# Dividing an attention's output instead of its weights, with sums from products with ones, and a retimed schedule, in a fused attention, delta-rule and feed-forward kernel

## The chip, the cores and the metric

The kernel runs on one core of one Trainium2 chip. A core has a matrix engine (PE, whose weight loads the profile shows as PEld), a vector engine (DVE), a scalar engine (ACT), a general engine (POOL), an engine that issues transfers (SP), and 16 DMA engines. The metric is device microseconds of one execution, the median over the runs; less is better.

## The reference

The input is 16 sequences of 128 tokens with 256 features. Two residual steps follow each other; all arithmetic is in float32.

```python
x = x + delta_rule(attention(x, cond_1, Wq, Wk, Wv, Wo), W_qkv, W_z, ...)
x = x + ffn(lora_ffn(x, Wg, Wu, Wd, adapters[itok]), gate_w, up_w, down_w, ...)

# attention: 16 heads of 16 features, causal
q, k, v = (proj(x, W) for W in (Wq, Wk, Wv))
q = q * minimum(cond_1, 4.0)
attn = softmax(where(causal, q @ k.T / sqrt(16), lowest), axis=-1)
return (attn @ v) @ Wo.T

# delta_rule: 16 key heads and 32 value heads of 128 features, chunks of 64 tokens:
# projections, a causal convolution of 4 taps, silu, norms of q and k, running sums of the
# gates, the inverse of a unit lower triangular 64 x 64 matrix per chunk and value head,
# values, outputs, a norm of the outputs, silu(z), and the product with W_out
```

The change lies in the softmax of `attention` and in the times at which the steps of all of the first residual step are placed.

## The kernel before

**Two levels of work.** The 16 sequences form 4 groups of 4 (`GS`). Attention (`attention`) runs on a group: `project` makes queries, keys and values, `block(g, i, e)` handles one sequence `i` and one half `e` of the features, which is 8 of the 16 heads, and `output` makes the group's result `hT`, its gates' logarithms (`logs`) and their running sums (`running`). There are 8 blocks in a group and 32 in all. The delta rule runs on 64 units, one for a key head and a group.

**One block.** `product` makes the scores of 8 heads in two PSUM tiles (L241). `mask` scales and masks them on DVE (L246), `largest` takes the maxima on DVE (L251), `less` subtracts them on POOL (L254), `exp` runs on ACT (L257). `total` sums the rows and takes reciprocals on DVE (L261, L262), and `share` divides the weights by multiplying them with those on POOL (L265). `turn` transposes the weights on PE by halves (L272) and copies them with ACT (L273). `weigh` multiplies values and weights (L280): four products of 32 columns each, which write the four blocks of 32 partitions of one PSUM tile. Each holds two heads, of which every partition needs one; `pick` chooses it with an ACT copy scaled by `even` and a DVE operation with `odd` (L287, L288).

**Times, and who obeys them.** Every step is a Python function with a time. Steps are sorted by time and called in this order, and then a scheduler of the framework, which has a model of durations of its own, makes each engine's instruction order from it. On the chip every engine takes its instructions strictly in that order. The unit of attention's times is one block: the steps of block b stand at b plus the twelve numbers of its list, for instance 2.2 for the first `turn`. Steps before `ALONE` = 11.2 run before anything else; the rest is spread over the first beats of the delta rule, `PACE` = 3.9 blocks to a beat. A beat is 24 units of the table `TIMES`; with each beat one new unit enters. A step at time t of `TIMES` runs in beat t // 24 after its unit entered, at t % 24.

**What is in a steady beat.** The steps of several units stand in one beat: `keys` of the newest (projections L437, convolution L446 and L448, SiLU L533, squares L469, norms L475), `decays` (L549, L553), `mergers` and `last` (which join the inverses of small blocks: L696 to L735), `values` (L437 again, L754), `outputs`: the gate (L771), `new_values` (L782, copied to `y` by ACT at L783), `attend` for two heads (L788, its square on ACT at L792, its product with the gate on DVE at L794) and `root` (L801, L803); and `finish` (POOL's L823, then L832 on PE). ACT's `exp` of `aT` stands at L511. For every four units `inverse` inverts 128 blocks of 32 by 32 on DVE and POOL, by rows (L587, L589), eights (L612, L616) and sixteens (L597 on POOL, L647 and L649 on DVE), spread over two beats. From beat 7 on the mergers and values need the memory that attention's tiles held, so attention ends before it.

**First loads.** SP's queue issues `wk`, the first group of `x` (`load_xT(0)`) and `wq` one after the other, ACT's queue the small ones.

The lines of the profile are those of this file:

Of the kernel before, what the change touches and what calls it, by code (L numbers as in the profile page):

```python
# [8 lines left out]
F32 = mybir.dt.float32  # L9
I32 = mybir.dt.int32  # L10
AF = mybir.ActivationFunctionType
ALU = mybir.AluOpType
AX = mybir.AxisListType
PSUM = bass.MemoryType.PSUM

P = 128
NB = 16
S = 128
D = 256
NT = NB * S  # L20
ND = D // P
NG = 4
GS = NB // NG
GT = GS * S
# [10 lines left out]
BL = 32  # L35
BLOCKS = tuple(slice(BL * b, BL * (b + 1)) for b in range(P // BL))
# [20 lines left out]
def tile_adaln_attn_ffn(  # L57
# [8 lines left out]
    nc = tc.nc  # L66
    V, A, G, T = nc.vector, nc.scalar, nc.gpsimd, nc.tensor
# [77 lines left out]
    HB = P // HD  # L145
    GB = GS * ND

    def attention():
# [22 lines left out]
        def load_xT(g):  # L171
            xTs[g] = p1.tile([P, ND, GT], F32, name="xT_sb", tag="xT")
            nc.sync.dma_start(out=xTs[g], in_=xT.rearrange("(c p) t -> p c t", p=P)[:, :, g * GT : (g + 1) * GT])

        nc.sync.dma_start(out=wk_sb, in_=wkT.rearrange("(c p) e -> p c e", p=P))
        load_xT(0)
        nc.sync.dma_start(out=wq_sb, in_=wqT.rearrange("(c p) e -> p c e", p=P))
        nc.scalar.dma_start(out=pr, in_=prec.rearrange("b o -> (b o)").partition_broadcast(P))
        nc.sync.dma_start(out=wv_sb, in_=wvT.rearrange("(c p) e -> p c e", p=P))
        nc.sync.dma_start(out=wo_sb, in_=woT.rearrange("(c p) e -> p c e", p=P))  # L180
# [50 lines left out]
        def block(g, i, e):  # L231
# [12 lines left out]
            def mask(n):  # L244
                b = g * GS + i
                V.scalar_tensor_tensor(out=d["s"][:, n], in0=d["ps"][n], scalar=pr[:, b : b + 1],  # L246
                                       in1=causal[:, None, :].to_broadcast([P, 4, S]), op0=ALU.mult, op1=ALU.add)
# [8 lines left out]
            def exp():  # L256
                A.activation(d["s"], d["s"], AF.Exp)  # L257

            def total():
                d["sm"] = p1.tile([P, HB], F32, name="sm", tag="sm")  # L260
                V.tensor_reduce(out=d["sm"], in_=wide(d["s"]), axis=AX.X, op=ALU.add)  # L261
                V.reciprocal(d["sm"], d["sm"])  # L262

            def share():
                G.tensor_tensor(wide(d["s"]), wide(d["s"]), d["sm"][:, :, None].to_broadcast([P, HB, S]), ALU.mult)  # L265

            def turn(n):
                if n == 0:
                    d["pT"] = p1.tile([P, 2, 4, S], F32, name="pT", tag="pT", bufs=1)
                ps = ps_b.tile([P, 4, S], F32, name="ps_pt", tag="b")  # L270
                for j in range(4):
                    T.transpose(ps[:, j, :], d["s"][:, n, j, :], ident)  # L272
                A.copy(d["pT"][:, n], ps)  # L273

            def weigh():

                d["po"] = ps_r.tile([P, 2, S], F32, name="ps_o", tag="r")
                for r, b in enumerate(BLOCKS):
                    c0 = e * P + r * BL
                    T.matmul(d["po"][b], lhsT=grp[g]["v"][:, i, c0 : c0 + BL],  # L280
                             rhs=d["pT"][:, r // 2, 2 * (r % 2) : 2 * (r % 2) + 2, :], start=True, stop=True)

            def pick():
                if i == e == 0:
                    grp[g]["oT"] = p1.tile([P, ND, GT], F32, name="oT", tag="oT", bufs=1)
                oT = grp[g]["oT"][:, e, cols]
                A.activation(oT, d["po"][:, 0, :], AF.Copy, scale=even)  # L287
                V.scalar_tensor_tensor(out=oT, in0=d["po"][:, 1, :], scalar=odd, in1=oT, op0=ALU.mult, op1=ALU.add)  # L288

            return [product, lambda: mask(0), lambda: mask(1), largest, less, exp, total, share,  # L290
                    lambda: turn(0), lambda: turn(1), weigh, pick]

        def output(g):

# [57 lines left out]
        def plan(t0, fs, times):  # L352
            steps.extend((t0 + t, len(steps) + i, f) for i, (t, f) in enumerate(zip(times, fs, strict=True)))

        for g in range(NG):
            t0 = GB * g
            plan(t0, project(g), [-2, -1.8, -1, -0.8, -0.6, -0.4] if g == 0 else [-6.55, -5.55, -4.55, -3.55, -2.85, -1.85])
            for i in range(GS):
                for e in range(ND):
                    plan(t0 + ND * i + e, block(g, i, e), [0, 0.15, 0.3, 0.45, 0.5, 1.0, 1.05, 1.45, 2.2, 2.45, 2.6, 2.8])  # L360
            plan(t0 + GB, output(g), [2.15, 2.45, 3.0, 3.6])
        return sorted(steps, key=lambda t: t[:2])


# [506 lines left out]
    def residual(g, t):  # L871
# [10 lines left out]
        "sums": [16.5],  # L882
        "decays": [42.5, 44.5, 48.5],
        "inverse": [4.0, 5.0, 6.0, 7.0, 8.0, 9.0, 10.0, 11.0, 12.0, 17.0, 17.0, 21.0, 23, 26, 25, 28, 27, 30, 29, 32, 34, 36, 36, 38, 38, 40, 40, 43, 46, 50],
        "mergers": [179, 180.5, 189.0],
        "last": [193.0],
        "values": [175.5, 179.5, 182, 186.5, 194, 195],
        "outputs": [217, 219, 224, 224, 227, 230, 232.5, 237],
        "finish": [244, 249.5, 255.5],
        "logs": [18],  # L890
    }
# [4 lines left out]
    LOG = TIMES["logs"][0]  # L896
    next_log = lambda name, i: int((TIMES[name][i] - LOG) // BEAT) + 1

    ALONE, PACE = 11.2, 3.9
    load_qk(units[0])  # L900
    ahead = attention()
    while ahead and ahead[0][0] < ALONE:
# [3 lines left out]
    def plan(n, steps, times):  # L906
        for f, t in zip(steps, times, strict=True):
            k = n + int(t // BEAT)
            planned.setdefault(k, []).append((t - BEAT * (k - n), len(planned[k]) if k in planned else 0, f))
# [279 lines left out]
```

## Time and profile before

| | |
|---|---|
| median of 3 runs | 2310.58 us (2308.94 to 2312.5) |
| the profiled execution: its time | 2318.2 us |
| its span, first to last instruction | 2316.5 us |
| busy: PE, DVE, ACT, POOL | 2137.0, 1360.2, 1363.9, 895.4 us |
| mean granted PE clock | 0.968 of full |
| first product of PE | at 12.15 us |
| first projection of unit 0 (beat 0 begins) | at 94.1 us |
| first merging product (L696) | at 316.6 us |

How to read it: busy times are unions of an engine's instructions, so four small products that run side by side count once. "idle before" is an engine's idle time ahead of an instruction, and the name after the arrow is what ended it. The clock column is the share of PE's clock that was granted; at 0.5 every product takes twice as long. An engine that is idle while another is the bound costs nothing.

### The profile page before, as it was taken

How to read it: one execution, taken by the hardware profiler on the slowest of the kernel's cores; microseconds unless marked ns; L12 is line 12 of the kernel's file. 1: busy time of each engine (PE TensorE's matmuls, PEld its weight loads, DVE VectorE, ACT ScalarE, POOL GpSimd, SP SyncE). 2: the span in 40 equal slices, each digit the busy share in tenths (PEclk: the TensorE clock that was granted, in tenths of full speed). 3: DMA queues.
4: the chain of work that ended last, by engine and by line, in shares of the span. 5: the costliest groups of instructions: out<-in, count | busy, mean ns of one | idle time of the engine just before them, and what ended most of it. 6: DMA issues, size and time to landing. Idle time of an engine off the chain costs nothing. (4 is left out here: it accounts for less than half of the span.)

```text
span 2316.5 us, 40743 instructions
## 1 busy us (share of the span) xinstructions
PE 2137.0 (92%) x15736; PEld 1295.8 (56%) x15736; DVE 1360.2 (59%) x2194; ACT 1363.9 (59%) x2359; POOL 895.4 (39%) x607
## 2 busy tenths in 40 slices
PE   6888669999999999999999999999987987999999
PEld 3444335666666666666666666566655663344445
DVE  4677778676676867768676676767665322211111
ACT  3666567777767777677777667677765561111110
POOL 3555635254252534525253452525454014500000
PEclk9899879999999999999999999999999898999999
DMA  2110123333334433333443333334333225000000
GB/s 59 52 58 20 28 67 91 106 89 103 93 99 108 113 104 97 96 100 90 116 110 99 102 95 100 88 104 114 96 97 102 77 62 159 0 5 16 9 0 18
DMA packets 303215, 182.11 MB, mean 79 GB/s; under 512 B 189360, under 2 KB 283312, under 8 KB 303024
## 3 DMA queue, kind: packets, MB, share of 16 engines
q1 hardware_dynamic: 301104, 175.27, 27.4%
q0 software_dynamic: 1344, 4.20, 0.6%
q8 instruction: 126, 2.06, 0.4%
q14 instruction: 65, 0.53, 0.1%
q10 hardware_dynamic: 576, 0.05, 0.0%
HBM read 152.69 MB, written 5.77 MB: 68 GB/s over the span
## 5 line engine op out<-in xcount | busy, mean ns | idle before, releaser
L448 DVE SCALAR_TENSOR_TENSOR cv<-ps_in,cw,cv 128x508 f32<-128x508 f32 (+2 forms) x768 | 559.6, 737 | 241.5 <-ACT cv L446 230.6
L832 PE MATMUL ps_out<-wo_head,z 128*128 128x256 f32 x1024 | 251.4, 390 | 36.0 <-POOL z L823 36.0
L823 POOL TENSOR_TENSOR z<-z,rb 128x1024 f32<-128x1024 f32 x64 | 151.0, 2360 | 333.1 <-DMA rb<-scales 332.9
L437 PE MATMUL ps_in<-hT,w_qk 128*128 128x512 f32 x512 | 248.7, 608 | 2.2 <-ACT qT L214 2.2
L771 PE MATMUL ps_z<-hT,w_gate 128*128 128x512 f32 x512 | 242.2, 595 | 0.0
L437 PE MATMUL ps_in<-hT,w_v 128*128 128x512 f32 x512 | 241.4, 592 | 0.0
L446 ACT ACTIVATE cv<-ps_in,cw 128x512 f32<-128x512 f32 x256 | 173.6, 684 | 114.1 <-PE ps_in L437 113.9
L832 PEld LDWEIGHTS ps_out<-wo_head,z 128*128 128x128 f32 x1024 | 190.3, 196 | 62.6 <-POOL z L823 40.5
L487 POOL TENSOR_TENSOR o<-off,lk 128x16 f32<-128x16 f32 x64 | 14.1, 220 | 439.7 <-ACT lk L517 425.0
L597 POOL TENSOR_TENSOR prod<-lanes,inv 128x512 f32<-128x512 f32 (+1 forms) x64 | 129.0, 2037 | 125.0 <-DVE inv L589 124.1
L794 DVE SCALAR_TENSOR_TENSOR z<-ps_ot,nw,z 128x512 f32<-128x512 f32 x128 | 95.2, 745 | 107.8 <-ACT sq L792 107.5
L788 PE MATMUL ps_ot<-aT,y 128*128 128x128 f32 x1024 | 143.8, 283 | 2.8 <-ACT y L783 2.8
L437 PEld LDWEIGHTS ps_in<-hT,w_qk 128*128 128x128 f32 x512 | 91.6, 190 | 96.7 <-issue 84.2
L549 PE MATMUL ps_kq<-kq 128*128 128x256 f32 x512 | 144.6, 429 | 0.0
L437 PEld LDWEIGHTS ps_in<-hT,w_v 128*128 128x128 f32 x512 | 92.3, 191 | 90.1 <-issue 81.5
L782 PEld LDWEIGHTS ps_y<-v,W 128*128 128x128 f32 x1024 | 124.4, 192 | 30.6 <-issue 29.8
L771 PEld LDWEIGHTS ps_z<-hT,w_gate 128*128 128x128 f32 x512 | 91.4, 190 | 87.5 <-issue 87.0
L788 PEld LDWEIGHTS ps_ot<-aT,y 128*128 128x128 f32 x1024 | 130.1, 192 | 11.9 <-ACT y L783 5.2
L533 ACT ACTIVATE kq<-cv 128x512 f32<-128x512 f32 x128 | 80.6, 630 | 94.5 <-DVE cv L448 94.4
L597 POOL TENSOR_TENSOR prod<-inv,gm 128x512 f32<-128x512 f32 (+1 forms) x64 | 128.2, 2031 | 0.0
L549 PEld LDWEIGHTS ps_kq<-kq 128*128 128x128 f32 x512 | 101.7, 210 | 44.4 <-PE ps_r L801 22.3
L782 PE MATMUL ps_y<-v,W 128*128 128x128 f32 x1024 | 124.6, 275 | 0.0
(207 smaller groups left out, 4136.1 us busy)
## 6 DMA issues: line engine op xcount, KB each, us to landing
aT<-sums SPq DMA_DIRECT2D x64, 512.0 KB
rb<-scales SPq DMA_DIRECT2D x64, 512.0 KB
w_qk<-in_w_qkv_dram SPq DMA_DIRECT2D x128, 128.0 KB
w_v<-in_w_qkv_dram SPq DMA_DIRECT2D x64, 256.0 KB
w_gate<-in_w_z_dram SPq DMA_DIRECT2D x64, 256.0 KB
wo_head<-in_w_out_dram SPq DMA_DIRECT2D x64, 256.0 KB
diag<-bT SPq DMA_DIRECT2D x256, 32.0 KB
W<-Uc SPq DMA_DIRECT2D x256, 32.0 KB
```

The source lines that it names most:

```text
L437: T.matmul(ps, lhsT=w[:, c, blk, :], rhs=hTs[g][:, c, :], start=c == 0, stop=c == ND - 1)
L446: A.activation(cv, psv, AF.Copy, scale=cw[:, col, 3:4])
L448: V.scalar_tensor_tensor(out=cv[:, :, sh:], in0=psv[:, :, : S - sh], scalar=cw[:, col, 3 - sh : 4 - sh], in1=cv[:, :, sh:], op0=ALU.mult, ...
L533: ins = A.activation(dst, src, AF.Silu)
L549: T.matmul(ps[:, j, :, :], lhsT=d["kq"][:, s, 0, :], rhs=d["kq"][:, s, :, :], start=True, stop=True)
L597: G.tensor_tensor(out_tile, lhs[:, :, None, :].to_broadcast([P, r, c, j]), rhs.rearrange("p j c -> p c j")[:, None, :, :].to_broadcast([P, ...
L771: T.matmul(ps, lhsT=w_gate[u][:, c, h * P : (h + 1) * P], rhs=hTs[g][:, c, :], start=c == 0, stop=c == ND - 1)
L782: T.matmul(ps[:, j, :], lhsT=d["W"][:, p, :], rhs=v[:, p, :], start=True, stop=True)
L788: T.matmul(ps[:, s * S : (s + 1) * S], lhsT=d["y"][:, 2 * s + h, :], rhs=d["aT"][:, 2 * s + h, :], start=True, stop=True)
L794: V.scalar_tensor_tensor(out=z, in0=ps, scalar=nw, in1=z, op0=ALU.mult, op1=ALU.mult)
L823: G.tensor_tensor(d["z"], d["z"], d["rb"], ALU.mult)
L832: T.matmul(ps[:, j, :], lhsT=d["z"][:, h, s * S : (s + 1) * S], rhs=w_o[u][:, h, :], start=kh == j == h == 0, stop=kh == NK - 1 and j == h ...
```

## The change

There are four edits.

The weights are no longer divided. `weigh` makes, beside the products with the values, the same four products with a tile of ones in place of the values, so that the lower half of the PSUM tile holds each head's sum of weights, already spread over the head's partitions. `pick` then chooses from values and sums at once (256 columns in place of 128), and `share`, now the block's last step, takes the reciprocal of the 128 chosen sums and multiplies, both on DVE. `total` and POOL's division go.

The first loads of `x` and `wq` are each issued as two halves of 128 rows, `wq` on ACT's queue, and `wk` comes after them.

Attention's lists of times get names and other numbers, and `PACE` becomes 4.1. As a block has eleven steps now, its list has eleven.

In `TIMES`, the third step of `mergers` (`grow`) moves from 189.0 to 188.5 and the fifth of `outputs` (`attend(0)`) from 227 to 225.

```diff
+        xTs[0] = p1.tile([P, ND, GT], F32, name="xT_sb", tag="xT")
+        for c in range(ND):
+            nc.scalar.dma_start(out=wq_sb[:, c], in_=wqT[c * P : (c + 1) * P])
+            nc.sync.dma_start(out=xTs[0][:, c], in_=xT[c * P : (c + 1) * P, 0:GT])
         nc.sync.dma_start(out=wk_sb, in_=wkT.rearrange("(c p) e -> p c e", p=P))
-        load_xT(0)
-        nc.sync.dma_start(out=wq_sb, in_=wqT.rearrange("(c p) e -> p c e", p=P))
...
-            def total():
-                d["sm"] = p1.tile([P, HB], F32, name="sm", tag="sm")
-                V.tensor_reduce(out=d["sm"], in_=wide(d["s"]), axis=AX.X, op=ALU.add)
-                V.reciprocal(d["sm"], d["sm"])
-
-            def share():
-                G.tensor_tensor(wide(d["s"]), wide(d["s"]), d["sm"][:, :, None].to_broadcast([P, HB, S]), ALU.mult)
...
             def weigh():
 
-                d["po"] = ps_r.tile([P, 2, S], F32, name="ps_o", tag="r")
-                for r, b in enumerate(BLOCKS):
-                    c0 = e * P + r * BL
-                    T.matmul(d["po"][b], lhsT=grp[g]["v"][:, i, c0 : c0 + BL],
-                             rhs=d["pT"][:, r // 2, 2 * (r % 2) : 2 * (r % 2) + 2, :], start=True, stop=True)
+
+                d["po"] = ps_r.tile([P, 2, 2, S], F32, name="ps_o", tag="r")
+                for k in range(2):
+                    for r, b in enumerate(BLOCKS):
+                        c0 = e * P + r * BL
+                        T.matmul(d["po"][b, k], lhsT=ones if k else grp[g]["v"][:, i, c0 : c0 + BL],
+                                 rhs=d["pT"][:, r // 2, 2 * (r % 2) : 2 * (r % 2) + 2, :], start=True, stop=True)
 
             def pick():
+                o = d["o"] = p1.tile([P, 2, S], F32, name="o_s", tag="o_s")
+                A.activation(o, d["po"][:, :, 0, :], AF.Copy, scale=even)
+                V.scalar_tensor_tensor(out=o, in0=d["po"][:, :, 1, :], scalar=odd, in1=o, op0=ALU.mult, op1=ALU.add)
+
+            def share():
                 if i == e == 0:
                     grp[g]["oT"] = p1.tile([P, ND, GT], F32, name="oT", tag="oT", bufs=1)
-                oT = grp[g]["oT"][:, e, cols]
-                A.activation(oT, d["po"][:, 0, :], AF.Copy, scale=even)
-                V.scalar_tensor_tensor(out=oT, in0=d["po"][:, 1, :], scalar=odd, in1=oT, op0=ALU.mult, op1=ALU.add)
+                V.reciprocal(d["o"][:, 1, :], d["o"][:, 1, :])
+                V.tensor_tensor(grp[g]["oT"][:, e, cols], d["o"][:, 0, :], d["o"][:, 1, :], ALU.mult)
...
-            return [product, lambda: mask(0), lambda: mask(1), largest, less, exp, total, share,
-                    lambda: turn(0), lambda: turn(1), weigh, pick]
+            return [product, lambda: mask(0), lambda: mask(1), largest, less, exp,
+                    lambda: turn(0), lambda: turn(1), weigh, pick, share]
...
-            plan(t0, project(g), [-2, -1.8, -1, -0.8, -0.6, -0.4] if g == 0 else [-6.55, -5.55, -4.55, -3.55, -2.85, -1.85])
+            plan(t0, project(g), FIRST_TIMES if g == 0 else PROJECT_TIMES)
             for i in range(GS):
                 for e in range(ND):
-                    plan(t0 + ND * i + e, block(g, i, e), [0, 0.15, 0.3, 0.45, 0.5, 1.0, 1.05, 1.45, 2.2, 2.45, 2.6, 2.8])
-            plan(t0 + GB, output(g), [2.15, 2.45, 3.0, 3.6])
+                    plan(t0 + ND * i + e, block(g, i, e), BLOCK_TIMES)
+            plan(t0 + GB, output(g), OUTPUT_TIMES)
...
-        "mergers": [179, 180.5, 189.0],
+        "mergers": [179, 180.5, 188.5],
...
-        "outputs": [217, 219, 224, 224, 227, 230, 232.5, 237],
+        "outputs": [217, 219, 224, 224, 225, 230, 232.5, 237],
...
-    ALONE, PACE = 11.2, 3.9
+    FIRST_TIMES = [-2, -1.8, -1, -0.6, -0.4, -0.2]
+    PROJECT_TIMES = [-6.8, -5.3, -4.3, -3.3, -2.6, -1.6]
+    BLOCK_TIMES = [0, 0.1, 0.25, 0.4, 0.55, 1.05, 1.55, 1.75, 2.35, 2.55, 2.75]
+    OUTPUT_TIMES = [2.1, 2.35, 3.0, 3.8]
+
+    ALONE, PACE = 11.2, 4.1
```

## The prediction

> **What bounds the kernel now.** I read the page's engine totals first, then a table of stretches, then the waits of TensorE (PE), then the timelines round its two long kinds of stall.
>
> ```profile
> span 2316.5 us, 40743 instructions
> PE 2137.0 (92%) x15736; PEld 1295.8 (56%) x15736; DVE 1360.2 (59%) x2194; ACT 1363.9 (59%) x2359; POOL 895.4 (39%) x607
> 12.10:94.10 82.00, 70.24 (x293) 34.95 (x294) 46.11 (x67) 40.65 (x67) 40.24 (x22) 0.90 0.07 20
> 94.10:249.00 154.90, 131.39 (x620) 65.89 (x619) 116.38 (x192) 109.09 (x173) 86.88 (x54) 0.93 0.14 47
> 249.00:309.60 60.60, 31.20 (x140) 16.75 (x139) 44.98 (x73) 31.62 (x45) 35.58 (x25) 0.77 0.10 27
> 363.90:1728.00 1364.10, 1317.84 (x11675) 862.89 (x11668) 970.40 (x1576) 980.27 (x1733) 598.16 (x411) 0.99 0.37 101
> 440.20:464.90 24.70, 24.29 (x222) 15.90 (x216) 18.48 (x38) 16.51 (x29) 11.52 (x9) 1.00 0.36 99
> 464.90:491.90 27.00, 24.08 (x223) 15.79 (x217) 22.51 (x35) 18.96 (x37) 19.30 (x12) 1.00 0.33 92
> ...
> 666.00:695.70 29.70, 26.79 (x218) 17.14 (x216) 23.32 (x37) 20.76 (x38) 21.86 (x14) 0.89 0.31 83
> ```
>
> After the span and the engines: a stretch, its length, busy us of PE, PEld, DVE, ACT and POOL, then the granted clock. PE is the bound. Between 364 and 1728 us it idles 46 of 1364 us. Before 310 us, where the first attention lies, it idles 12 + 12 + 24 + 29 = 77 us and is granted 0.77 to 0.93 of its clock. So there are two places to win or lose: attention's stretch, and the one beat in four (27 us or more, others about 24) that holds most of an inverse.
>
> ```profile
> PE ps_pt L272 <- POOL sc L265: 28.8, 9, 6.8
> PE ps_sums L337 <- DVE gd L330: 19.0, 3, 17.5
> PE ps_qk L200 <- DMA wq_sb<-in_wqT_dram: 12.2, 1, 12.2
> ...
> 303.04 0.80 PE L337 MATMUL ps_sums<-tri,gd 128*128 128x128 f32 x2 [17.52 <-DVE gd L330]
> ...
> 475.70 1.95 PE L782 MATMUL ps_y<-v,W 128*128 128x128 f32 x16
> 477.48 1.89 PE L832 MATMUL ps_out<-wo_head,z 128*128 128x256 f32 x8
> 479.21 1.05 PE L788 MATMUL ps_ot<-aT,y 128*128 128x128 f32 x8
> 488.35 0.64 PE L801 MATMUL ps_r<-sq,ones 128*32 128x256 f32 x8 [2.92 <-ACT sq L792]
> ...
> 482.14 0.63 ACT L533 ACTIVATE kq<-cv 128x512 f32<-128x512 f32 x1 [3.15 <-DVE cv L448]
> 488.19 1.05 ACT L511 ACTIVATE aT<-aT 128x1024 f32<-128x1024 f32 x1
> ...
> 472.39 1.22 DVE L647 TENSOR_REDUCE gm<-prod 128x64 f32<-128x1024 f32 x1 [2.44 <-POOL prod L597]
> ```
>
> The first three rows (total, times, longest) say what PE waits for before 345 us: the division of the weights on POOL, the last group's logarithms, the first loads. The rest is one slow beat: PE waits 2.92 us for the second square on ACT; ACT was late because its SiLU waited for the convolution on DVE, which stood behind a reduction whose product POOL had not finished.
>
> **First loads.** `wq` leaves SP's third place for ACT's queue, and `x` goes in halves ahead of `wk`. Now 1.4 MB (cw, w_qk, wk, x, wq) are asked for before the first product can run at 12.15 us. Afterwards its first half needs only one half of each, and `wk` no longer stands ahead: 0.64 MB fewer, some 4 us at the 180 to 270 GB/s that flow then. ACT's `pr`, `dtb` and `nega` are issued two issues (0.9 us) later, covered by the first 12 us. I take -3.5 us (-1 to -5.5); `wk` itself comes next and is wanted four passes later.
>
> **Attention, per block (32).** Removed: POOL's division, 1.90 us; DVE's sum, 1.22, its reciprocal of 8, 0.19, and its pick of 128, 0.34. Added: four products with ones on PE, a pick of 256 on ACT and DVE, a reciprocal of 128 and a product of 128 on DVE.
>
> ```profile
> L280 PE MATMUL ps_o<-pT,vt 128*32 128x256 f32 x256 | 29.7, 411 | 6.6 <-ACT pT L273 6.3
> L801 PE MATMUL ps_r<-sq,ones 128*32 128x256 f32 x512 | 41.5, 396 | 39.9 <-ACT sq L792 39.1
> L262 DVE RECIPROCAL sm<-sm 128x8 f32<-128x8 f32 x32 | 6.2, 192 | 0.1
> L288 DVE SCALAR_TENSOR_TENSOR oT<-ps_o,rowf,oT 128x128 f32<-128x128 f32 x32 | 11.0, 343 | 11.9 <-ACT oT L287 11.9
> ```
>
> PE: the same shape as L280 and L801, where four column tiles run together: 256 passes of 411 ns are only 29.7 us busy, and a set of eight goes by in 0.45 us (488.35 to 488.80). So about 0.5 us a block, 16 us in all, 14 of it before beat 5. It lies on PE's own path: +14 (8 to 20).
>
> DVE: the nearest row is the reciprocal of 8 at 192 ns. A small DVE operation takes 144 ns, so 6 ns an element: 0.144 + 128 x 0.006 = 0.9 us. [...] I keep the row's slope. DVE is 75% busy in 94 to 249, and these steps end a block while the next ones are under way: I cost them at nothing, the cover being PE's 5 us a block; without it up to +10. ACT: 256 for 128 costs some 0.1 us a block, and the built order has three more table loads (1.28 us each), all beside PE.
>
> The chain of a block loses DVE's sum and POOL's division (3.3 us and two queues), so the transposes wait for `exp`. At the start this is plain: mask, maximum, `less` and `exp` end at 31.56, so the transposes run at 31.6 and not at 35.68: -4, and with a gap of 2 us in place of 6.13 half of the half-rate stretch after it, -2. Of the later waits on the division up to beat 5 (14.2 us) I take half, since the transposes are also planned nearer to `exp` (0.5 of a step, was 1.2) and DVE is no emptier: -7 (0 to -14). Less throttling there: -3. POOL's FIFO is 1.9 us a block shorter for `less` and the fades of the units; that is in these terms.
>
> **Pace.** 4.1 steps a beat for 3.9 put one more block before beat 5: +5, paid back after it. There, now, the last group's sums stand behind DVE's inverse rows, while PE holds them at the head of its queue: 17.5 us. In the built order of the changed kernel they stand before beat 6's projections, and the logarithms stand between the first reductions of the inverse, not behind all of it. From the end of the rows (269.7) to the first merging product (316.6) takes 47 us now. Walked with the same durations: product on POOL 3.0, reduction 1.2, product 3.0, reduction and logs 2.1 (gd at +9.3), then the sixteens, 5 + 2.4 + 2.3 + 5 us with their reductions, and a transpose, 1.93: the inverse ends near +34, with POOL's two pairs of memsets between, +1.5. So -11.5 (-2 to -16).
>
> Attention's stretch: -3.5 + 14 - 4 - 2 - 7 - 3 + 5 - 11.5 = -12.
>
> **Every beat after (54).** `attend(0)` moves from 11 to 9 of 24. PE's order becomes: new values, two of its four products, one of four `ps_out`, two, three `ps_out`. The second half needs the second copy of `y`; behind it in PE's queue stand three `ps_out` and the second projection of the values, and ACT's square waits for it. In usual beats that copy ends 0.75 us after the new values do, plus 0.1 to be seen; PE gets there after 0.45 + 0.43 us less the 0.16 by which ends are modelled late: a stall of 0.12, in 40 beats: +5. Nothing hides it, as PE is the bound. (The four `ps_out`, 1.73 us, hide it now.)
>
> In the 14 slow beats the built order also differs: a reduction whose product is long ready (L647 of Tc) stands ahead of the one that DVE waits 2.44 us for, so the second tap of the convolution isn't behind it. First SiLU 1.9 us earlier, second (482.14) near 480.2. Against it, ACT's `exp` of `aT`, now after the second square (488.19), stands before it: +1.05. Walking ACT's queue: SiLU, squares 1.06, square, SiLU after its last tap at 482.1, table 1.28, `aT` 1.05, copy, two of 0.39, then the second square ends at 487.5 in place of 488.29. So -0.75 x 14 = -10.5. Were `aT` itself not ready (POOL's fade), the copy and the second square behind it would wait too; the fade ends at 469.5, 15 us before. `grow` half a unit earlier passes one reduction of the inverse: free. In these beats the order on SP's and POOL's queues is unchanged; in beats 6 to 8 SP issues five loads of weights (0.5 us each) ahead of the first placements of `W` and `T`, which still wait for the inverse then: nothing.
>
> Throttle: 7 of the 14 slow beats show a clock of 0.89 or 0.94 and last 1 to 2.7 us over 27; 13.5 us in all. Stalls of 1.9 us never show it, those of 2.9 in about half. [...]
>
> Steady beats: +5 - 10.5 - 6 = -11.5 (-25 to +8).
>
> **Sum.** -12 - 11.5 = -23.5, with a little for shorter POOL queues at beat 5: -25 on the profiled execution's 2318.2 (span 2316.5 and 1.7 round it). That run is 7.6 over the median of 2310.6; the difference carries over: 2285.6.
>
> **Rivals.** (1) Steady beats win nothing (the convolution's order gives back what `aT` takes): attention's -12 and half of the last stall's, 2299. For: ACT is full from the SiLU to the square; against: DVE's wait of 2.44 us is plainly avoided. [...] (3) Slower: PE waits for `y`. If ACT's copies come as in the slow beats (1.34 us after the new values) in every beat, the stall is 0.7 us x 54 = 38, against -12 and half of -16: +18, 2329. It decides from about 0.5 us a beat. Against it: they come so in 16 beats, all behind the late SiLU. (4) Attention at PE's floor, stalls all gone: -30 there, -20 later: 2260. (5) The division may be off the path altogether, and nothing moves: 2310.
>
> **Numbers.** Forecast 0.50 (2270 to 2299), rivals (1) 0.12, (2) 0.10, (3) 0.14, (4) 0.07, (5) 0.07. 0.2% is 4.6 us, about what a measurement of this kernel can tell from no change. Faster: 0.50 + 0.12 + 0.10 + 0.07 = 0.79 less 0.01 of their edges = 0.78; same 0.08; slower 0.14. Range 2262 to 2312: it leaves out most of (3), half of (4).
>
> **What would show it.** PE starts by 9 us; transposes wait for ACT's `exp`, under 15 us in all; beat 0 near 85 us; `ps_sums` waits under 8 us; the first merge near 303; slow beats near 26.3 us with the wait on `sq` near 2.2; usual beats 24.1; reciprocal near 0.9. Wrong if `ps_ot` waits for `y` by over 0.5 us a beat, or if the first merge is no earlier.

## The result, and the profile after

The changed kernel takes 2281.99 us (median of 4 runs, 2279.25 to 2287.56) against 2310.54 us (4 runs beside them): a ratio of 0.9879, with a 95% interval of 0.9859 to 0.9899, or 28.6 us less. The forecast was 2285.6. The total is near, but its two parts are both far from their forecast, on opposite sides: in the profiled executions the stretch up to the first merge wins 36.1 us where 12 were predicted, and the steady beats win nothing where 11.5 were predicted.

The profiled execution took 2279.25 us. First two lines of its page, then the stretches that answer to those of before (length, busy us of PE, PEld, DVE, ACT and POOL, granted clock):

```profile
span 2277.5 us, 41217 instructions
PE 2133.1 (94%) x15992; PEld 1289.1 (57%) x15992; DVE 1370.0 (60%) x2194; ACT 1365.9 (60%) x2362; POOL 834.5 (37%) x575
```

```profile
8.53:83.80 75.27, 68.31 (x385) 34.03 (x385) 47.53 (x83) 42.89 (x71) 20.86 (x11) 1.00 0.13 39
83.80:227.20 143.40, 132.20 (x806) 68.20 (x803) 119.74 (x197) 122.72 (x185) 53.11 (x35) 0.98 0.16 51
227.20:280.53 53.33, 34.53 (x137) 17.45 (x135) 45.43 (x77) 23.91 (x36) 33.06 (x26) 0.84 0.25 67
...
404.90:430.20 25.30, 24.52 (x226) 15.89 (x217) 18.66 (x38) 15.98 (x29) 11.39 (x9) 1.00 0.35 98
430.20:456.20 26.00, 24.09 (x222) 15.75 (x216) 22.30 (x35) 18.96 (x35) 19.00 (x11) 1.00 0.36 95
...
356.50:1666.80 1310.30, 1271.11 (x11241) 826.24 (x11232) 939.27 (x1514) 936.53 (x1662) 566.64 (x389) 0.99 0.37 101
```

The first three stretches are attention alone (up to beat 0), beats 0 to 4, and from beat 5 to the first merging product; then come a beat ahead of a slow one, a slow one, and the 52 beats from unit 11 to unit 63. From the table of stretches of before, the third and the last of these, with the same ends:

```profile
249.00:316.60 67.60, 38.20 (x157) 19.62 (x155) 50.60 (x81) 34.93 (x50) 39.66 (x29) 0.80 0.14 34
392.00:1700.70 1308.70, 1265.93 (x11239) 829.56 (x11233) 928.22 (x1515) 942.43 (x1668) 568.49 (x389) 0.99 0.37 101
```

PE is still the bound, with almost the same busy total (2133.1 for 2137.0) although it runs 256 products more. Attention alone is shorter by 6.7 us, beats 0 to 4 by 11.5, the way from beat 5 to the first merge by 14.3; the first product comes 3.6 us earlier (8.53). The 52 beats take 1310.3 us for 1308.7.

The waits of PE before 345 us (total, times, longest), and then the groups of two new operations (busy, mean ns of one, idle before):

```profile
PE ps_n L475 <- ACT sqa L469: 13.1, 3, 7.2
PE ps_pt L266 <- ACT sc L259: 11.3, 8, 3.1
PE ps_qk L202 <- DMA xT_sb<-in_xT_dram: 9.4, 2, 8.5
PE ps_sums L337 <- DVE gd L330: 7.8, 1, 7.8
```

```profile
L276 PE MATMUL ps_o<-pT,ones 128*32 128x256 f32 x256 | 24.0, 381 | 0.0
...
L287 DVE RECIPROCAL o_s<-o_s 128x128 f32<-128x128 f32 x32 | 30.4, 949 | 0.6
```

The 28.8 us in which the transposes waited for POOL's division are 11.3 us for ACT's exponentials. The wait for the last sums fell from 17.5 to 7.8 us, but part of it returns one step later, as a wait for `sqa` of 7.2 us.

Where the 36.1 us lie can be worked out from these rows: idle is length less PE's busy time, and busy time times one less the clock is an estimate of what the throttle took. The slow first products (experiment 1) show a clock of 1.00, so they count as work here.

| us, after less before | first product | attention alone | beats 0 to 4 | beat 5 to first merge | sum |
|---|---|---|---|---|---|
| PE idle | -3.6 | -4.7 | -12.3 | -10.6 | -31.2 |
| lost to the clock | | -7.0 | -6.6 | -2.1 | -15.7 |
| work at full clock | | +5.1 | +7.4 | -1.6 | +10.9 |
| length | -3.6 | -6.7 | -11.5 | -14.3 | -36.1 |

After the first merge the profiled runs differ by little more: +2 us up to unit 63, and -5 in the tail behind it. That last piece can't be put down to the change: the tail from unit 63 on takes 615.8 us in before's profile and 610.7 in the changed kernel's, and between 605.7 and 616.6 in the profiles of the experiments. In all the two profiled runs lie 39 us apart and the medians 28.6, because the one is 7.6 us above its median and the other 2.7 below. The first merge itself comes out alike when its code is run again: at 317.1 and 318.4 us in experiments 1 and 2, for 316.6, and at 280.8 in experiment 4, for 280.5.

### The profile page after: what moved, and what is told of

The parts are those of the page before. It is cut to its first block, busy times and chain, and to the rows that moved or that the text cites. A ratio compares the mean times of both kernels' runs of the same rounds, so it can differ in the third digit from the quotient of the medians.

```text
span 2277.5 us, 41217 instructions
## 1 busy us (share of the span) xinstructions
PE 2133.1 (94%) x15992; PEld 1289.1 (57%) x15992; DVE 1370.0 (60%) x2194; ACT 1365.9 (60%) x2362; POOL 834.5 (37%) x575
## 5 line engine op out<-in xcount | busy, mean ns | idle before, releaser
L448 DVE SCALAR_TENSOR_TENSOR cv<-ps_in,cw,cv 128x500 f32<-128x500 f32 (+2 forms) x768 | 559.5, 738 | 284.4 <-ACT cv L446 273.1
L832 PE MATMUL ps_out<-wo_head,z 128*128 128x256 f32 x1024 | 259.5, 389 | 33.4 <-POOL z L823 33.4
L832 PEld LDWEIGHTS ps_out<-wo_head,z 128*128 128x128 f32 x1024 | 185.5, 195 | 55.9 <-POOL z L823 37.1
L788 PE MATMUL ps_ot<-aT,y 128*128 128x128 f32 x1024 | 160.0, 290 | 4.3 <-ACT y L783 3.9
L437 PEld LDWEIGHTS ps_in<-hT,w_v 128*128 128x128 f32 x512 | 96.9, 191 | 93.2 <-issue 79.0
L794 DVE SCALAR_TENSOR_TENSOR z<-ps_ot,nw,z 128x512 f32<-128x512 f32 x128 | 95.4, 747 | 51.8 <-ACT sq L792 51.5
L491 POOL TENSOR_TENSOR aT<-aT,o 128x1024 f32<-128x1024 f32 x64 | 121.8, 1902 | 7.0 <-DMA aT<-sums 1.3
L514 ACT ACTIVATE r<-r 128x256 f32<-128x256 f32 x64 | 26.7, 416 | 161.3 <-DVE r L803 161.3
```

Of the source, the lines that this page charges most:

```text
L437: T.matmul(ps, lhsT=w[:, c, blk, :], rhs=hTs[g][:, c, :], start=c == 0, stop=c == ND - 1)
L448: V.scalar_tensor_tensor(out=cv[:, :, sh:], in0=psv[:, :, : S - sh], scalar=cw[:, col, 3 - sh : 4 - sh], in1=cv[:, :, sh:], op0=ALU.mult, ...
L491: G.tensor_tensor(t4, t4, o.rearrange("p s h i -> p (s h) i")[:, :, :, None].to_broadcast([P, NP, 2, C]), ALU.subtract)
L788: T.matmul(ps[:, s * S : (s + 1) * S], lhsT=d["y"][:, 2 * s + h, :], rhs=d["aT"][:, 2 * s + h, :], start=True, stop=True)
L794: V.scalar_tensor_tensor(out=z, in0=ps, scalar=nw, in1=z, op0=ALU.mult, op1=ALU.mult)
L832: T.matmul(ps[:, j, :], lhsT=d["z"][:, h, s * S : (s + 1) * S], rhs=w_o[u][:, h, :], start=kh == j == h == 0, stop=kh == NK - 1 and j == h ...
```

## The experiments

Each was measured beside the kernel before, on one of four chips; intervals are 95%. In the table "us" is the ratio's distance from 1 times 2310.5, since the kernel before has medians from 2311.7 to 2321.9 us on these chips. "Beat 9" is the start of unit 9's first projection in the profiled run, 341.6 us before. It is not adjusted for the chip, and a profile shows one execution: those of experiments 8 and 10 are 10.5 us under and 13.4 us over the median of their kernel.

| kernel | ratio | interval | us | beat 9 |
|---|---|---|---|---|
| changed | 0.9879 | 0.9859 to 0.9899 | -28.0 | 305.9 |
| 1 loads alone | 0.9994 | 0.9983 to 1.0006 | -1.4 | 340.6 |
| 2 late times alone | 1.0006 | 0.9996 to 1.0015 | +1.4 | 342.0 |
| 3 softmax alone, old times | 0.9916 | 0.9898 to 0.9934 | -19.4 | 323.0 |
| 4 changed, old late times | 0.9873 | 0.9854 to 0.9892 | -29.3 | 309.5 |
| 5 changed, old block times | 0.9916 | 0.9895 to 0.9937 | -19.4 | 327.0 |
| 6 changed, pace 3.9 | 0.9911 | 0.9890 to 0.9932 | -20.6 | 320.4 |
| 7 changed, ones twice | 0.9937 | 0.9917 to 0.9957 | -14.6 | 327.3 |
| 8 changed, idle POOL work, free | 1.0039 | 1.0028 to 1.0051 | +9.0 | 349.7 |
| 9 changed, no reciprocal | 0.9892 | 0.9876 to 0.9907 | -25.0 | 316.9 |
| 10 times alone, old softmax | 1.0036 | 1.0023 to 1.0049 | +8.3 | 353.0 |
| 11 changed, idle POOL work, bound | 0.9886 | 0.9861 to 0.9910 | -26.3 | 316.6 |
| 12 changed, pace 4.3 | 0.9928 | 0.9907 to 0.9948 | -16.6 | 319.9 |

The theory was: the softmax's shorter chain to the transposes wins the time, PE pays for the ones, and the new times cash in what the chain leaves. Its rivals: the loads or the late times carry a part; POOL's lighter queue is what helps; the times help by themselves; DVE is at its limit.

**1. The first loads alone.**

```diff
 (kernel before)
+        xTs[0] = p1.tile([P, ND, GT], F32, name="xT_sb", tag="xT")
+        for c in range(ND):
+            nc.scalar.dma_start(out=wq_sb[:, c], in_=wqT[c * P : (c + 1) * P])
+            nc.sync.dma_start(out=xTs[0][:, c], in_=xT[c * P : (c + 1) * P, 0:GT])
         nc.sync.dma_start(out=wk_sb, in_=wkT.rearrange("(c p) e -> p c e", p=P))
-        load_xT(0)
-        nc.sync.dma_start(out=wq_sb, in_=wqT.rearrange("(c p) e -> p c e", p=P))
```

> The kernel before with only the first loads changed: the group's activations and the query weights by halves, the latter on ACT's queue, the key weights behind them. The loads end early by what TensorE's first product shows: it begins near 8.5 us as in the profile after (12.15 before), and if this lead is kept to the end the time is 3.5 to 4 us below before. If the key weights, now last, hold up the second projection, the lead is eaten in the first beat: then beat 0 is no nearer its end than before and the time is within 1 us of before. Nothing of the 36 us that the profile after gains up to the first merge should come from here beyond these 4.

The first product did come at 8.56 us, but the time is that of before. The timeline of PE in this kernel (start, length, products, the wait ahead of them) shows why; the third group is at 17.61 in the kernel before:

```profile
8.56 2.08 PE L202 MATMUL ps_qk<-xT_sb,wq_sb 128*128 128x512 f32 x2 [8.56 <-DMA xT_sb<-in_xT_dram]
11.69 2.08 PE L202 MATMUL ps_qk<-xT_sb,wq_sb 128*128 128x512 f32 x2 [1.06 <-DMA xT_sb<-in_xT_dram]
13.56 2.65 PE L202 MATMUL ps_qk<-xT_sb,wk_sb 128*128 128x512 f32 x4
16.05 1.88 PE L202 MATMUL ps_qk<-xT_sb,wq_sb 128*128 128x512 f32 x4
```

Of the lead of 3.6 us, 1.06 goes to a wait for the second half of `x`. A further 1.0 goes to slow products: the first ones take some 1.04 us each, and here six or so of them do, where before it was about three (3.75 us for the first four). 1.56 us are left at 16.05, and 1.1 where beat 0 begins (92.94 for 94.07). That is below what these runs can tell from nothing: the interval ends at -3.9 and +1.4 us.

**2. The two late times alone.**

```diff
 (kernel before)
-        "mergers": [179, 180.5, 189.0],
+        "mergers": [179, 180.5, 188.5],
-        "outputs": [217, 219, 224, 224, 227, 230, 232.5, 237],
+        "outputs": [217, 219, 224, 224, 225, 230, 232.5, 237],
```

> The kernel before with only two late times changed: the third merger at 188.5 in place of 189.0 and the fifth output at 225 in place of 227. The prediction's sum says -11.5 us (slow beats down to 26.3, ordinary beats up by 0.1). The theory from the profile after says that the beats from unit 11 to unit 63 lose as much as they win: ordinary beats 24.0 to 24.2, the beat before a slow one 24.7 to 25.3, slow beats 27.0 to 26.0; so the time is within 4 us of before, and the first merge begins at 316 us as before.

Nothing is won: the interval ends at -0.9 and +3.5 us. From its profile, an ordinary beat, the beat ahead of a slow one, and a slow one, and PE's waits from unit 11 to unit 63:

```profile
392.60:416.80 24.20, 24.20 (x227) 15.76 (x216) 16.08 (x24) 17.41 (x32) 6.11 (x7) 1.00 0.38 102
441.00:466.40 25.40, 24.62 (x227) 15.92 (x217) 18.56 (x38) 16.11 (x29) 11.37 (x9) 1.00 0.36 97
466.40:492.30 25.90, 24.12 (x220) 15.74 (x217) 22.32 (x35) 18.98 (x36) 18.96 (x11) 1.00 0.36 95
```

```profile
PE ps_r L801 <- ACT sq L792: 29.6, 13, 2.7
PE ps_up L709 <- DVE cv L448: 4.0, 10, 0.4
PE ps_up L708 <- DVE z L794: 3.6, 10, 0.4
```

This slow beat wins 1.1 us of its 27.0, the two ordinary ones give back 0.2 each, and the beat between, 24.7 before, gives back 0.6 to 0.7. Part of the last is a new wait of 0.36 us in ten beats: the merging products L708 wait for DVE's L794, which was not on PE's path before. Ten of the 13 slow beats still last over 26.5 us here.

**3. The softmax alone, at the times of before.** The changed kernel with the loads, late times, pace and step times of before; its list for a block is the old one without the two steps that go:

```diff
 (changed kernel; loads, late times and the other lists of times as before)
-    BLOCK_TIMES = [0, 0.1, 0.25, 0.4, 0.55, 1.05, 1.55, 1.75, 2.35, 2.55, 2.75]
+    BLOCK_TIMES = [0, 0.15, 0.3, 0.45, 0.5, 1.0, 2.2, 2.45, 2.6, 2.8, 2.9]
...
-    ALONE, PACE = 11.2, 4.1
+    ALONE, PACE = 11.2, 3.9
```

> The kernel before with only the softmax changed: sums as products with ones, the division at the output; the loads, the late times, the pace of 3.9 and the times of the steps are those of before (a block's turns stay at 2.2 and 2.45, the division comes at 2.9). Theory A, the chain: the gain up to the first merge comes from the shares leaving the path (28.8 us of waits for them), whatever the times; then the first merge begins 20 to 30 us earlier than before's 316.6 and the time is 15 to 25 us below. Theory B, the times: without the new times the ones' products (24 us busy) and the division come on top, TensorE has as much to do and the turns wait in their old places; then the first merge begins within 8 us of before and the time is from 5 us below to 10 us above.

The softmax wins 19.4 us without any new time; the first merge comes 17.6 us earlier, at 299.0, for the 20 to 30 expected. Its stretches (attention alone, beats 0 to 4), and from its waits that of the transposes:

```profile
12.15:84.80 72.65, 68.86 (x365) 33.85 (x364) 43.34 (x64) 41.31 (x67) 20.86 (x11) 0.98 0.07 21
84.80:240.70 155.90, 136.44 (x773) 68.23 (x772) 116.47 (x189) 116.73 (x177) 51.99 (x34) 0.96 0.14 47
```

```profile
PE ps_pt L264 <- ACT sc L257: 5.0, 2, 2.9
```

With the turns planned as late as before, they wait 5.0 us in all, so the chain was what they waited for. Attention alone falls from 82.0 to 72.7 us, ones included.

**4. The changed kernel with the late times of before.**

```diff
 (changed kernel)
-        "mergers": [179, 180.5, 188.5],
+        "mergers": [179, 180.5, 189.0],
-        "outputs": [217, 219, 224, 224, 225, 230, 232.5, 237],
+        "outputs": [217, 219, 224, 224, 227, 230, 232.5, 237],
```

> The changed kernel with the two late times of before (third merger at 189.0, fifth output at 227). If the late times bring the 11.5 us of the prediction, this is slower than the changed kernel by about that: 2293. If they bring nothing on balance, as the profile after reads, it is within 4 us of 2282; ordinary beats are then back at 24.0 and slow ones at 27.0.

2283.3 us (4 runs), a ratio within 0.0006 of the changed kernel's: the late times bring nothing here either. Its ordinary beats are 24.0 us again and its slow ones 27.0 or more.

**5 and 6. One of the new times taken back.** Experiment 5 has the old list for a block (as in 3), experiment 6 the old pace; all else is the changed kernel's.

```diff
 (5)
-    BLOCK_TIMES = [0, 0.1, 0.25, 0.4, 0.55, 1.05, 1.55, 1.75, 2.35, 2.55, 2.75]
+    BLOCK_TIMES = [0, 0.15, 0.3, 0.45, 0.5, 1.0, 2.2, 2.45, 2.6, 2.8, 2.9]
 (6)
-    ALONE, PACE = 11.2, 4.1
+    ALONE, PACE = 11.2, 3.9
```

> The changed kernel with only the old times of a block's steps: the turns at 2.2 and 2.45 and the division at 2.9, in place of 1.55, 1.75 and 2.75; pace, projection times, loads and late times are the changed kernel's. If the turns' place in the order is what the softmax's shorter chain is cashed in by, the stretch up to the first merge loses 8 to 15 us against the changed kernel (280.5) and the time is 2290 to 2297. If the chain was already short enough for the old places, the time is within 4 us of 2282 and what is left of the step times' gain belongs to the pace and the projections.

> The changed kernel with only the old pace of 3.9 blocks a beat. The prediction put +5 us on the faster pace as extra load (more blocks a beat), and so expects 2277 or so here. The reading of the profile after is the reverse: beats 1 to 4 take 28 to 29 us with four blocks each as with 3.9, and the faster pace ends attention's tail a quarter of a beat sooner; then the first merge begins 5 to 10 us later than 280.5 and the time is 2287 to 2292.

Either one taken back costs some 8 us (the intervals just touch that of the changed kernel) and leaves what the softmax brings alone. In the profiles the first merge comes at 301.9 and 295.8 us, later than expected. The waits of PE before 345 us, two rows of experiment 5 and then four of 6:

```profile
PE ps_n L475 <- ACT sqa L469: 19.5, 4, 13.4
PE ps_sums L337 <- DVE gd L330: 10.7, 1, 10.7
```

```profile
PE ps_pt L266 <- ACT sc L259: 15.7, 6, 4.6
PE ps_sums L337 <- DVE gd L330: 14.6, 1, 14.6
PE ps_o L276 <- ACT pT L267: 12.6, 9, 3.5
PE ps_n L475 <- ACT sqa L469: 5.3, 3, 2.9
```

In both the last sums wait longer than the 7.8 us of the changed kernel. In experiment 5 the norms `ps_n` do too (19.5 us for 13.1). In experiment 6 they wait less (5.3), and the blocks' own products more: 15.7 us for 11.3 in `ps_pt`, 12.6 for 4.7 in `ps_o`.

**7. The products with ones twice.**

```diff
 (changed kernel)
-                for k in range(2):
+                for k in (0, 1, 1):
```

> The changed kernel with every product with ones issued twice: 256 more products of 381 ns on one column tile, 24 us of TensorE's summed busy time, in a stretch where TensorE is busy more than nine tenths. The prediction's +14 us for the ones says the same again here: 2296. If the column tiles run beside each other (four at a time), 32 blocks x 8 products cost about a quarter of the sum, 6 us, and the time is 2288. If they lie in TensorE's waits, nothing: within 4 us of 2282.

The groups of L276 in this kernel:

```profile
L276 PE MATMUL ps_o<-pT,ones 128*32 128x256 f32 x512 | 39.2, 393 | 0.0
L276 PE MATMUL ps_o<-pT,vt 128*32 128x256 f32 x256 | 26.9, 408 | 4.0 <-ACT pT L267 3.9
```

256 products more are 15.2 us of busy time (39.2 less 24.0), and the time rises by 13.4 us (0.9937 against 0.9879; the intervals do not meet, but together they leave some 6 us either way). So PE's busy time for the ones is paid, and the ones of the change should cost about that much as well. The expectation's 6 us came from a misreading: the 24 us of L276 are a union already, in which products side by side count once (their sum is 256 x 0.381 = 98 us), so no quarter of it was to be taken.

**8. POOL's work given back, off the chain.**

```diff
 (changed kernel)
+        spare = w1.tile([P, 256], F32, name="spare")
+        G.memset(spare, 1.0)
...
                 A.activation(d["s"], d["s"], AF.Exp)
+                for _ in range(4):
+                    G.tensor_tensor(spare, spare, spare, ALU.mult)
```

> The changed kernel with POOL given back the work that the shares took from it, but off the chain: after each block's exponential is issued, four multiplications 128x256 of a tile that nothing else reads (together about as long as the 1.9 us of a share). If POOL's relief is what brings the time, the gain goes: first merge 10 to 30 us after 280.5 and a time of 2292 to 2310. If it is the shorter chain (reduction 1.22, reciprocal 0.19 and share 1.90 us out of the way from the exponential to the turn), the time is within 4 us of 2282.

The tile of this multiplication depends on no block, and the framework's scheduler put all 128 of them early. The tile's row, and then the stretches of attention alone and of beats 0 to 8:

```profile
L263 POOL TENSOR_TENSOR spare<-spare x128: 602/613/747, 2.4 to 104.0; 128x256 f32<-128x256 f32 x128
```

```profile
8.53:127.80 119.27, 83.09 (x384) 40.62 (x384) 48.61 (x83) 43.33 (x71) 94.72 (x133) 0.83 0.08 25
127.80:349.70 221.90, 185.66 (x1173) 97.60 (x1169) 183.99 (x304) 167.53 (x254) 90.70 (x65) 0.93 0.19 56
```

79 us of POOL's time stood ahead of beat 0, which begins 44 us later; from there to beat 9 it takes 221.9 us for the changed kernel's 222.1. So this does not answer the question: it says that a queue crowded at the start holds up attention's start, not what a share's time a block costs. Experiment 11 asks again.

**9. Without the reciprocal.**

```diff
 (changed kernel)
+        even_share = w1.tile([P, S], F32, name="even_share")
+        G.memset(even_share, 1 / 64)
...
-                V.reciprocal(d["o"][:, 1, :], d["o"][:, 1, :])
-                V.tensor_tensor(grp[g]["oT"][:, e, cols], d["o"][:, 0, :], d["o"][:, 1, :], ALU.mult)
+                V.tensor_tensor(grp[g]["oT"][:, e, cols], d["o"][:, 0, :], even_share, ALU.mult)
```

> The changed kernel without the reciprocal: the attention's output is multiplied by a constant in place of one over its sum, so DVE has 32 instructions of 0.95 us (30 us) less and all else stays. The rival that DVE takes over as the bound says that these 30 us are nearly on the path: 10 to 25 us less than 2282. The prediction's sum, which costs the reciprocal at nothing beside TensorE, says within 4 us of 2282.

-25.0 us against before, where the changed kernel has -28.0, with intervals that overlap: 30 us less of DVE's work win nothing, where the rival expected 10 to 25 us. The order of the instructions differs too, which may be why beats 0 to 4 take 152.0 us here for the changed kernel's 143.4; that was not followed up. So a gain of some 8 us could be hidden here, and the run speaks against DVE as the bound without excluding that its work costs something.

**10. The new times with the old softmax.**

```diff
 (kernel before)
-            plan(t0, project(g), [-2, -1.8, -1, -0.8, -0.6, -0.4] if g == 0 else [-6.55, -5.55, -4.55, -3.55, -2.85, -1.85])
+            plan(t0, project(g), [-2, -1.8, -1, -0.6, -0.4, -0.2] if g == 0 else [-6.8, -5.3, -4.3, -3.3, -2.6, -1.6])
-                    plan(t0 + ND * i + e, block(g, i, e), [0, 0.15, 0.3, 0.45, 0.5, 1.0, 1.05, 1.45, 2.2, 2.45, 2.6, 2.8])
-            plan(t0 + GB, output(g), [2.15, 2.45, 3.0, 3.6])
+                    plan(t0 + ND * i + e, block(g, i, e), [0, 0.1, 0.25, 0.4, 0.55, 1.05, 1.1, 1.5, 2.2, 2.4, 2.55, 2.75])
+            plan(t0 + GB, output(g), [2.1, 2.35, 3.0, 3.8])
-    ALONE, PACE = 11.2, 3.9
+    ALONE, PACE = 11.2, 4.1
```

> The kernel before with its own softmax (reduction, reciprocal and share ahead of the turns), but the new times of projections and output, the pace of 4.1, and the new times of a block as far as they fit: the turns stay behind the share at 2.2 and 2.4. If the times bring a gain by themselves, whatever the softmax, this is 5 to 12 us below before, about what the changed kernel lies under the one with the new softmax at old times. If the times only cash in the shorter chain, it is within 4 us of before or slower, since more blocks a beat then wait for the same chain.

8.3 us slower than before. The stretch of beats 0 to 4, and the wait of the transposes, in the slowest execution of the 14:

```profile
100.80:273.40 172.60, 141.84 (x641) 69.09 (x640) 121.16 (x198) 122.46 (x185) 90.89 (x55) 0.88 0.13 42
```

```profile
PE ps_pt L272 <- POOL sc L265: 37.6, 12, 6.7
```

The times ask for more blocks a beat than the long chain delivers: the shares are waited for 37.6 us (28.8 before), and the clock falls to 0.88 (0.93). The new pace, with as much of the new lists as fits, costs 8 us here; with the loads (1.4 us or so), the new times win some 9 us behind the short chain.

**11. POOL's work given back, bound to its block.**

```diff
 (changed kernel)
+        spare = w1.tile([P, 2, S], F32, name="spare")
...
                 A.copy(d["pT"][:, n], ps)
+                for j in ((), (0, 1, 2))[n]:
+                    G.tensor_tensor(spare, d["s"][:, n, j : j + 2, :], d["s"][:, n, j : j + 2, :], ALU.mult)
```

> The changed kernel with POOL given back the work that the shares took from it, but off the chain, and this time bound to its block: with the second turn, three multiplications 128x256 that read the exponentials and write a tile that nobody reads (3 x 0.61 = 1.84 us a block, as a share's 1.90), so that they can't gather at the start; they stand in POOL's queue between two blocks' subtractions as the shares did. If POOL's queue is what the change relieves, the gain of 20 us that the softmax brings at old times goes: 2300 or more, and the transposes wait again for exponentials whose subtraction is late. If it is the shorter chain to the turn (1.22 + 0.19 + 1.90 us less), the time is within 4 us of 2282.

From 84 to 280 us of this kernel POOL's two largest groups, and the wait of the transposes up to 345 us:

```profile
L270 POOL TENSOR_TENSOR spare<-sc 128x256 f32<-128x256 f32 x66 | 40.7, 616 | 31.1 <-ACT sc L260 25.8 <-DVE turned L481 2.0
L257 POOL TENSOR_TENSOR sc<-sc,mx 128x1024 f32<-128x1024 f32 x21 | 39.8, 1896 | 29.0 <-DVE mx L254 27.0 <-PE ps_sc L244 1.9
```

```profile
PE ps_pt L267 <- ACT sc L260: 14.4, 10, 3.3
```

POOL is as loaded as it was before, with a wait for each exponential between two subtractions, and 26.3 of the 28.0 us stay. Its lighter queue is a small part of the gain: 1.7 us, with the two intervals at most some 9. The first merge comes at 289.6 us for 280.5, but on a chip where the kernel before takes 11 us more. With POOL's load (11), the loads (1), the late times (2, 4) and the times by themselves (10) ruled out as its main part, and DVE's load no lower than before (1370.0 us busy for 1360.2), the shorter chain is what remains, and experiment 3 shows the new softmax acting without the new times. How much of it is DVE's sum and how much POOL's division was not taken apart.

**12. A faster pace still.**

```diff
 (changed kernel)
-    ALONE, PACE = 11.2, 4.1
+    ALONE, PACE = 11.2, 4.3
```

> The changed kernel with a pace of 4.3 blocks a beat. From 3.9 to 4.1 the time fell by some 7 us, since attention's last steps left the beat after unit 6. If a beat still has room, 4.3 brings the last output earlier again and the first merge 2 to 6 us: 2276 to 2280. If TensorE and DVE are full in beats 1 to 4 (28 us with DVE busy 0.83 of the time), the beats grow by what the tail wins, and the time is 2280 to 2288.

11 us slower than the changed kernel, worse than the worst expected. Beats 0 to 4:

```profile
84.40:241.30 156.90, 139.67 (x830) 70.57 (x827) 125.85 (x203) 122.19 (x186) 55.11 (x36) 0.95 0.15 46
```

They take 13.5 us more than in the changed kernel: 6.0 are idle time of PE, 4.3 the clock by the estimate above, and 3.1 work that now stands earlier. The way from beat 5 to the first merge is no shorter for it (53.4 us for 53.3), as `ps_n` waits 16.6 us. 4.1 is better than its neighbours on both sides, though the interval of 3.9 just touches its own. None of the versions is faster than the changed kernel by more than its interval.

## Why the prediction was right, and where it was not

The direction, and the main cause as the prediction had it (a chain without DVE's sum and POOL's division), held. The sum came near because its errors cancel: some 24 us too little up to the first merge, 11.5 too much behind it, and the rest in where the single profiled executions lie about their medians. So the nearness of the total is luck. By its own steps:

- **First loads, -3.5.** The first product came 3.6 us earlier, as costed. That this reaches the end is not seen: 1.1 us of it are left at beat 0, and the time gains 1.4 us with an interval from -3.9 to +1.4 (experiment 1). The step let the first half start without asking when the second half arrives.
- **Ones, +14.** Held: 10.9 us of work by the table (up to the first merge PE runs 258 products more, 1328 for 1070, of which 256 are the ones), and 13.4 for the same set once more (experiment 7). That small products in four column tiles go by at about a quarter of their sum (24.0 us busy for 98 in L276) was rightly read from the row of L280.
- **DVE at nothing.** Nothing speaks against it (experiment 9, with its reserve). The reciprocal of 128 took 949 ns, where the slope from the row of 8 gave 0.9 us. With the pick of 256 (0.48 us) and the product (0.41 us, where L330 took 0.28 before for the same shape) that is 1.84 us a block for the 1.75 removed, so DVE has 3 us more to do up to the end of attention.
- **First turn -4, other shares -7, the last sums -11.5.** PE's idle time in these places fell by 27.7 us for a predicted 22.5. Beat 0 begins 10.3 us earlier, at 83.8 for a forecast of 85. The last stretch was walked well: rows' end to first merge took 37.7 us (242.8 to 280.5) where 46.9 less 11.5, or 35.4, was forecast. The wait for the last sums fell to 7.8 us; 7.2 us for `sqa` came up behind it.
- **Throttling -5.** A large miss: -15.7 by the table. The step counted only the half-rate stretch after the first turn and 3 us for all others. But up to 345 us the kernel before has 12 waits of PE of 1.9 us or more (the first loads left aside), and 11 of them were followed by the half rate within 3.41 us; the changed kernel has six, of which four were. The step went by the length of a stall, from the slow beats; the length alone does not decide (last section).
- **Pace +5.** Wrong in sign. One block more before beat 5 was counted as a cost up to the first merge, though the same block had to be done before it anyway. Put back to 3.9, the kernel loses 7 us (experiment 6). Against the old softmax the step would have had the right sign (experiment 10, pace and lists together).
- **Steady beats -11.5.** Failed: nothing (experiments 2 and 4). Its pieces, over the 52 beats from unit 11 to 63 in the profiles before and after:
  - Moving `attend(0)` costs 9.2 us in the 39 beats that are not slow, 0.24 each, where +5 at 0.12 was forecast. It lies at the place that was named: in beat 12 the second projection of the values begins 4.60 us after the new values (391.50 to 396.10), and 4.40 before (426.97 to 431.37). The trace lists no idle time there, so whether it is the wait for `y` is not shown.
  - The 13 beats ahead of a slow one lose another 3.2 us, which the sum did not have: the first L708, which now waits for L794, comes 4.3 us later, in all, behind the products ahead of it, 0.6 follow in its group, and 1.7 are won back between. The walk went through PE's and ACT's queues and stopped before these last products of the beat.
  - Slow beats win 10.7 us, for -10.5 and -6 of throttling. No run shows those 6, an estimate of about half of the 13.5 us that the prediction counts in beats at a lower clock: 7 of the 13 still last over 26.5 us.

Rival 1, that the steady beats win nothing, is what happened there; rival 4, attention rid of its stalls for -30, is near what happened before them. Rivals 3 and 5 fell: what the moved `attend(0)` costs, 0.24 us a beat, is under the 0.5 from which rival 3 decides (PE's listed waits for `y` are 1.2 us in three places); attention did win, and the division was on the path. DVE as the bound (rival 2) would have left attention nothing, and experiment 9 speaks against it.

Not settled: why `ps_n` waits so long behind attention's end at a pace of 4.3. A version with sums on DVE off the chain, which would spare PE the ones, was not tried.

## What to carry to other kernels

When a chain between two uses of the bounding engine gets shorter, count the clock as well as the wait: here each microsecond of idle time that went brought about half a microsecond of throttled time with it (15.7 for 27.7, the one an estimate). A schedule's times are worth what the chain behind them allows: the faster pace with its lists cost 8 us with the long chain, won some 8 with the short one, and lost again one step further, so retune after a structural change and test the times apart from it. And follow a moved step to the end of its beat: what it wins in the beat that you look at may be waited for in the one before.

## What was unexpected of the hardware

Short stalls cost the clock more than the slow beats had suggested, and their length alone does not decide. In the kernel before, PE waited 2.17 us from 101.75 and 1.94 from 114.61, and both waits were followed by products at half the clock. In the changed kernel a wait of 2.77 us from 90.39 was, but one of 3.12 from 26.46 was not. At half the clock PE's work goes by half as fast: in the changed kernel four products of 128x512 take 3.78 us from 95.16, at 0.50, and 1.88 from 100.74, at 1.00.

In every profile here the granted clock changes only at the points of a grid of 3.41 us. Rows that follow this grid show what happens (length, busy us of PE, PEld, DVE, ACT and POOL, then the clock), first two pairs of before, then the two waits of the changed kernel:

```profile
101.41:104.83 3.42, 1.25 (x4) 0.49 (x3) 1.69 (x3) 1.80 (x3) 0.90 (x1) 1.00 0.00 0
104.83:108.24 3.41, 3.41 (x11) 2.17 (x10) 3.38 (x9) 2.86 (x4) 1.84 (x1) 0.50 0.11 34
...
115.07:118.48 3.41, 1.60 (x16) 0.45 (x16) 1.13 (x2) 3.40 (x7) 2.93 (x2) 1.00 1.01 395
118.48:121.89 3.41, 3.41 (x11) 1.63 (x8) 3.00 (x7) 2.24 (x5) 2.31 (x3) 0.50 1.01 414
```

```profile
24.60:28.01 3.41, 1.86 (x4) 0.56 (x4) 3.34 (x5) 0.00 (x0) 1.46 (x1) 1.00 0.27 89
28.01:31.42 3.41, 1.83 (x12) 1.16 (x12) 1.02 (x1) 2.67 (x5) 2.33 (x2) 1.00 0.00 0
31.42:34.84 3.42, 3.42 (x26) 1.63 (x25) 2.97 (x4) 1.95 (x3) 0.26 (x1) 1.00 0.02 5
...
89.45:92.86 3.41, 0.94 (x2) 0.11 (x2) 3.34 (x7) 1.71 (x3) 1.90 (x1) 1.00 0.00 0
92.86:96.28 3.42, 3.12 (x4) 1.10 (x5) 2.42 (x7) 2.65 (x4) 0.00 (x0) 0.50 0.16 55
```

The wait of 1.94 us falls with other gaps into one step of the grid, in which PE is busy 1.60 of 3.41 us, and the next step runs at 0.50. The wait of 3.12 is divided between two steps that are busy 1.86 and 1.83 us, and costs nothing. A count of all steps at full clock in the fourteen profiles agrees: where PE was idle for over 60% of a step, the next was at half clock in all 254 cases; where it was idle for less than half, in 9 of 8515; between the two both happen (40 of 114). In the profiles before and after alone it is all of 36, none of 1211, and 5 of 16. So it is the idle share of a single step that counts here, and the same stall can be free or not by where it lies. The grid is not tied to the program's start: from run to run its points lie elsewhere (those of the rows of before and of the changed kernel by half a step).
